# A shorter least time per unit in the clock that orders a four-layer kernel, and a bank kept for the front chain

## The chip, the cores and the metric

The kernel runs on one core of one Trainium2 chip. The metric is the device time of one execution in microseconds (us). A core has five engines that work side by side, each taking its instructions from a queue of its own: TensorE (PE in the profile; its weight loads are PEld), VectorE (DVE), ScalarE (ACT), GpSimd (POOL) and SyncE (SP, which here only issues DMAs).

## The reference

The input `x` is four images of 96 channels and 64 x 64 pixels. Four layers follow one another; each adds its result to what it got.

- Layer 0: group norm, layer norm, a projection to 2 x 192 channels, a 3 x 3 depthwise convolution, and then a selective scan over the 4096 pixels in four directions (rows, columns, and both backwards), with a state of 16 values per channel: `h = dA * h + d_t * u_t * b_t`, `y = sum(h * c_t)`. The four results are added, normed, multiplied by a gate and projected back to 96 channels.
- Layer 1: group norm and a deformable 3 x 3 convolution. A convolution gives for each pixel and tap an offset and a mask; the image is sampled there bilinearly (four corners), weighted, and multiplied by the 3 x 3 weights.
- Layer 2: over tokens, an FFT block (up to 192 channels, a transform over 4096 tokens, a product, ReLU, the inverse transform, and down to 96 channels), then a feed-forward block whose numbers are rounded to 8 bits.
- Layer 3: linear attention with six heads, and another such feed-forward block.

The recurrence is the heart of it: in `selective_scan` the state of each of 4 images x 4 directions x 192 channels x 16 values is carried through 4096 steps.

## The kernel before, in words

**The scan.** VectorE has an instruction that runs a recurrence along a row. The kernel cuts the work into 1536 *units*: for each image `b` and direction `k`, four pieces of 1024 pixels (`T`), and for each piece 24 units of eight channels x 16 state values on the 128 partitions. Images are taken one after the other; in images 1 to 3 the directions come in the order 1, 3, 0, 2, so that an image's last quarter is direction 2. A unit consists of: a load `da` of the step sizes (`fetch`, on ScalarE's DMA queue, five units ahead), their exponential (`decay`, L1014, ScalarE), two matmuls that spread the inflow into `db` in PSUM (`inflow`, L1020, TensorE), a product of `db` with `bc` (`enter`, L1034, VectorE), the scan into `hh` (`recur`, L1042, VectorE), a product of `hh` with the other half of `bc` (`weigh`, L1051, GpSimd), and matmuls that sum over the state into `py` (`total`, L1070, TensorE, for two units at a time). `py` is copied to `yb` and stored to DRAM as `y`.

**The side streams.** All else is written as Python generators that yield one *step* at a time, with its price for TensorE, VectorE, ScalarE and GpSimd. Two streams run beside the scan:

- `ends`: what comes before the scan and after sampling. It makes the scan's inputs for image 0 (`first`), then for images 1, 2 and 3 (`before`: convolution, projection, and `steps`, which makes step sizes and inflow), and then takes images 0 to 3 through layers 2 and 3 (`Layers23.image`; its store of `out` is L1833). An image enters layers 2 and 3 when `middle` has sampled it. `before(b)` has to be ready before the scan takes image `b`.
- `middle`: for each image `behind` (adds the directions of the scan, norm, gate, projection; it waits for the units of directions 3 and 2 that it reads, starts with L1134 on GpSimd and ends with L1180 and L1189), then `Layer1.image`: offsets and positions, and `sample`, which gathers 288 times from a table with GpSimd's indirect DMA (L1383), weighs the corners, transposes (L1416), multiplies by the weights and stores `x2` (L1439).

**Who sets the order.** The order is decided while the program is built, and each engine then runs its queue in that order. A `Clock` keeps for each engine a modelled time `ends[engine]`, and a scheduled time `due` of the scan. After each unit, `unit` adds `PACE` to `due`:

```python
    def now(self):
        return max(self.ends[DVE], self.due) if self.own is None else self.own

    def unit(self, scanned):
        self.due += PACE
        self.idle, self.beside = max(scanned, self.due), 0.0
```

Between two units the streams put in steps, `middle` before `ends` until the last image is sampled, for as long as `has_room` says that each engine of the step is at most `AHEAD` = (3, 3, 5, 7) us (PE, DVE, ACT, POOL) ahead of `now`, and while the VectorE work put beside a unit is under 6 us. When neither stream has a step that fits, the next unit is issued. A unit's own prices are 0.5 us for `inflow` and, for each two units, 1.5 us for `total` on TensorE (1.3 more for each eighth unit), 1.22 + 2.33 us on VectorE, 1.15 us on ScalarE for the exponential and 2.55 us on GpSimd; a gather is priced at 1.5 us of GpSimd. Where the inputs of the next image are not made yet, or when all units are over, a second mode (`alone`) takes steps without the scan.

Within a stream most stages are *pipelines*: `pipe` holds several chains (one for each chunk of pixels, say) in the order of their start and takes a step of the first chain that can go. The first of them is `active[0]`, the *front*. Three banks of PSUM are shared by the side streams while the scan runs (the scan has the other five); a step says with `holds` how many banks it keeps past its end, and with `new` that the next step will take a bank. `has_bank` asks whether one is free. After the scan its five banks become the own banks of `ends` (`own_banks`).

Of the kernel before, what the change touches and what calls it, by code (L numbers as in the profile page):

```python
# [186 lines left out]
def wait(us=0.0, **more):  # L187

    return Step((0.0,) * 4, us, **more)
# [10 lines left out]

MARGIN = 0.5

PACE = 4.5


class Clock:
# [19 lines left out]
# [4 lines that stand above are left out]
# [42 lines left out]
def pipe(net, chains, width, every=0, lane=None, **tiles):  # L272


    chains, active = iter(chains), []
    clock, known, more = net.clock, net.known, True
    end, free = clock.now(), tiles
    while True:
        if more and len(active) < width:
            steps = next(chains, None)  # L280
            if steps is None:
                more = False
            else:
                active.append(Chain(steps, clock.now()))
                continue
        if not active:
            break
        for n, chain in enumerate(active):
            if chain.new and not net.has_bank():
                continue  # L290
            if any(
                a.done <= chain.done + every
                for a in active[:n]
                if lane is None or (a.kind is lane) == (chain.kind is lane)
            ):
                continue
            if not all(free[tag] > 0 for tag in chain.takes):
                continue
            if clock.has_room(known.get((chain.kind, chain.done), (1.0,) * 4), chain.ready):
                break  # L300
        else:
            yield BLOCKED
            continue
        for tag in chain.takes:
            free[tag] -= 1
        clock.precede(known.get((chain.kind, chain.done), (0.0,) * 4))
        step = next(chain.steps, None)
        if step is None:
            net.hold(-chain.holds)
            active.remove(chain)  # L310
            end = max(end, chain.ready)
            continue
        for tag in step.frees:
            free[tag] += 1
        known[chain.kind, chain.done] = step.work
        chain.ready = clock.queue(step, chain.ready)
        chain.done += 1
        net.hold(step.holds - chain.holds)
        chain.holds, chain.new, chain.takes = step.holds, step.new, step.takes
        yield None  # L320
    yield wait(max(0.0, end - clock.now()))
# [38 lines left out]
class Net:  # L360
# [39 lines left out]
        own = self.own_banks and self.stream.own  # L400
        return (self.own_banks if own else self.psum).tile([128, CH], F32, name=name, tag="mm")[:p]

    def has_bank(self):
        if self.own_banks:
            return self.stream.held < (5 if self.stream.own else 3)
        return sum(stream.held for stream in self.streams) < 3

    def hold(self, n):
        self.stream.held += n
# [63 lines left out]
    def centred(self, x, cen, dst, key, pool, bias=None, groups=(0, 1)):  # L473
# [36 lines left out]
        def chains():  # L510
            for r in groups:
                for q in range(4):
                    yield chain(4 * r + q)
                yield sums(r)

        yield from pipe(self, chains(), 5, every=-99, sq=4, v0=-3, v1=-3)
        rstd = pool.tile([128, CH], F32, name=f"lns{key}", tag="lns", bufs=1)
        nw = pool.tile([128, CH], F32, name=f"lnw{key}", tag="lnw", bufs=1)
# [36 lines left out]
class Layer0:  # L555
# [54 lines left out]
    def first(self):  # L610
# [5 lines left out]
        with tc.tile_pool(name=f"l0u{b}", bufs=1) as up, tc.tile_pool(name=f"l0b{b}", bufs=1) as sm:  # L616
# [5 lines left out]
            with tc.tile_pool(name=f"l0a{b}", bufs=1) as big, tc.tile_pool(name=f"l0i{b}", bufs=1) as cp:  # L622
                pad = big.tile([C, PW, PW], F32, name=f"pad{b}", tag="pad")
                weights = self.conv_weights(b, cp)
                yield from self.normed_rows(b, x, pad)

                def rows_first():
                    yield self.conv(b, 0, pad, us, weights, cp)
                    for j in range(NCH):
                        if j + 1 < NCH:  # L630
                            yield self.conv(b, j + 1, pad, us, weights, cp)
                        yield self.projected(b, j, us, xp_a, xp_c, sm, xdbl, (0,), f"c{j}")
                        for ks in ((0,), (0, 2), (2,)):
                            yield self.steps(b, ks, j, us, dtw, sm, xdbl)

                tokens = {f"c{j}": 0 for j in range(NCH)}
                yield from pipe(
                    net, rows_first(), 6, every=2, lane=Layer0.conv.__code__,
                    ex=3, lw=2, rl=2, du=2, zt=1, **tokens,
                )  # L640

            def columns():
                for j in range(NCH):
                    yield self.projected(b, j, us, xp_a, xp_c, sm, xdbl, (1,))
                    for ks in ((1,), (1, 3), (3,)):
                        yield self.steps(b, ks, j, us, dtw, sm, xdbl)

            yield from pipe(net, columns(), 5, every=2, ex=3, lw=2, rl=2, du=2)

    def before(self, b):  # L650
# [1208 lines left out]
def layers23(net, x2, out):  # L1859
# [4 lines left out]
    with ExitStack() as ctx:  # L1864
# [37 lines left out]
        for goes in l0.scan():  # L1902
# [3 lines left out]
            if clock.own is not None:  # L1906
                clock.due = max(clock.due, clock.own + PACE)
                clock.idle = max(clock.idle, clock.due)
# [32 lines left out]
```

## Time and profile before

| what | value |
|---|---|
| time, median of three runs | 8518.56 us (8506.89 to 8540.53) |
| the profiled execution | 8585.65 us, of which its span is 8582.9 us |
| mean granted TensorE clock | 0.786 |
| busy: TensorE, VectorE, ScalarE, GpSimd | 76%, 79%, 57%, 65% of the span |
| first and last scan | 183 us and 7487 us |
| DMA: bytes, mean rate | 1608 MB, 187 GB/s |

The profiled execution is 0.8% above the median of the runs; its rows are used for durations and for the order of things. In a row of a group, the number after the bar is the busy time of all its instructions, then the mean duration of one in ns, then the idle time of the engine just before them and what ended most of that. In a row of waits, the numbers are the total in us, how often, and the longest. In a row of a timeline, the numbers are the start and the duration in us. In a row of a stretch, they are the ends of the stretch, its length, and the busy time of each engine with the number of instructions in brackets.

### The profile page before, as it was taken

The page shows a single profiled execution, that of the slowest core. Times are in us where ns is not written, and L with a number is a line of the kernel's source. Part 1 is how long each engine was busy: PE and PEld are TensorE (multiplying, and loading weights), DVE is VectorE, ACT ScalarE, POOL GpSimd, SP SyncE. Part 2 cuts the span into 40 slices and gives each one's busy share as a digit, 9 for nine tenths or more (in the row PEclk, how much of TensorE's full clock was granted, in tenths as well). Part 3 has the DMA queues.
Part 4 walks back from the last instruction along what each step waited for, and adds up shares of the span by engine and source line. Part 5 has one row for each costly group of instructions (what it writes and reads, how often), then busy time and mean ns, then how long its engine had stood idle before and what let it go on. Part 6 is the DMA issues. An engine that isn't in the chain of part 4 may idle for free.

```text
span 8582.9 us, 96776 instructions
## 1 busy us (share of the span) xinstructions
PE 6491.0 (76%) x31814; PEld 2822.5 (33%) x31848; DVE 6815.3 (79%) x5122; ACT 4923.9 (57%) x8979; POOL 5616.1 (65%) x4308
## 2 busy tenths in 40 slices
PE   6775877679767668777767889777788777887487
PEld 2211221122222223311223555214454332464274
DVE  2799889888799888688898888888888887727614
ACT  5664566546567767755566667554667774423124
POOL 1565567656579888666688887675788986517600
PEclk9766877679668779877777888778788877888698
DMA  3677678868789888876788989777898886734410
GB/s 97 168 198 193 167 196 221 212 159 204 189 215 249 224 228 222 202 190 187 205 229 225 235 227 228 172 174 188 223 243 219 210 212 168 176 103 131 131 56 20
DMA packets 773929, 1608.29 MB, mean 187 GB/s; under 512 B 264081, under 2 KB 355757, under 8 KB 771222
## 3 DMA queue, kind: packets, MB, share of 16 engines
q10 hardware_dynamic: 244224, 843.17, 38.4%
q1 hardware_dynamic: 455478, 532.37, 24.0%
q0 software_dynamic: 73728, 226.57, 9.9%
q8 instruction: 255, 4.18, 0.2%
q14 instruction: 244, 2.00, 0.1%
HBM read 1345.43 MB, written 256.29 MB: 187 GB/s over the span
## 4 chain that ended last, share of the span: by engine, by line
PE 35%; DVE 30%; DMA 9%; issue 9%; ACT 9%; POOL 4%; SPq 1%; ACTq 1%; another core or an unknown queue 1%; DVEq 0%; POOLq 0%
DVE hh L1042 15%; DVE db L1034 8%; PE pc L763 4%; PE py L1070 4%; PE ps L1416 3%; PE f L1510 3%; POOL hh L1051 3%; ACT g L1395 2%; PE pd L1432 2%; PE db L1020 2%; DMA da<-de 2%; ACT da L1014 2%; PE h L1551 1%; PE zp L1576 1%; DMA m<-in_dft 1%
## 5 line engine op out<-in xcount | busy, mean ns | idle before, releaser
L1051 POOL TENSOR_TENSOR hh<-hh,bc 128x1024 f32<-128x1024 f32 x1536 | 3670.2, 2391 | 348.3 <-DVE hh L1042 230.6
L1042 DVE TENSOR_TENSOR_SCAN hh<-da,st,db 128x1024 f32<-128x1024 f32 x1152 | 2701.3, 2345 | 205.3 <-PE py L1070 68.5
L1034 DVE TENSOR_TENSOR db<-db,bc 128x1024 f32<-128x1024 f32 x1536 | 1863.1, 1213 | 561.7 <-PE db L1020 542.2
L1014 ACT ACTIVATE da<-da,w_al 128x1024 f32<-128x1024 f32 x1536 | 1736.9, 1145 | 496.0 <-DMA da<-de 144.5
L1383 POOL DMA_INDIRECT g<-table,idx x1152 | 1190.6, 1034 | 410.9 <-issue 185.9
L1020 PE MATMUL db<-du,rep 24*128 24x512 bf16 x3072 | 697.7, 453 | 802.4 <-DVE hh L1042 752.2
L1070 PE MATMUL py<-hh,w_fold 128*32 128x512 f32 x6144 | 1115.9, 786 | 30.9 <-POOL hh L1051 18.0
L1395 ACT ACTIVATE g<-g,wt 128x96 f32<-128x96 f32 x3456 | 965.0, 364 | 133.5 <-PE py L1070 38.9
L1042 DVE TENSOR_TENSOR_SCAN hh<-da,db 128x1024 f32<-128x1024 f32 x384 | 877.1, 2284 | 73.9 <-PE py L1070 23.6
L1416 PE MATMUL ps<-w_ident,g 128*96 128x128 f32 x3744 | 690.5, 331 | 246.3 <-issue 122.2
L1020 PEld LDWEIGHTS <-rep 24*128 24x128 bf16 x3072 | 160.3, 93 | 1914.3 <-issue 1278.0
L851 POOL TENSOR_TENSOR lw<-lw,w 128x512 f32<-128x512 f32 x192 | 244.1, 1272 | 710.9 <-DVE w L849 668.5
L1416 PEld LDWEIGHTS ps<-w_ident,g 128*96 128x96 f32 x3744 | 501.6, 149 | 594.1 <-issue 211.2
L1049 POOL COPY st<-hh 128x1 f32<-128x1 f32 x1152 | 234.6, 204 | 648.4 <-DVE hh L1042 612.7
L763 PE MATMUL pc<-pad,wc 96*128 96x512 f32 x1152 | 570.8, 632 | 8.8 <-ACT st L1424 2.6
L1424 ACT COPY st<-ps 96x384 f32<-96x384 f32 x384 | 180.3, 472 | 578.9 <-PE ps L1416 421.5
L882 PE MATMUL pr<-ex,w_ident 128*128 128x512 f32 x384 | 299.7, 872 | 146.7 <-DVE ex L872 57.1
L840 PE MATMUL pd<-xd,w_dtw 103*64 103x512 f32 (+1 forms) x512 | 281.5, 818 | 71.2 <-DVE rl L853 26.9
L1432 PE MATMUL pd<-st,wdc 96*128 96x256 f32 x1152 | 323.0, 434 | 11.6 <-ACT st L1424 4.2
L763 PEld LDWEIGHTS pc<-pad,wc 96*128 96x128 f32 x1152 | 217.2, 199 | 311.8 <-issue 291.0
L1519 ACT COPY d<-f 128x512 f32<-128x512 f32 x192 | 111.3, 582 | 315.2 <-PE f L1510 282.3
L1070 PEld LDWEIGHTS py<-hh,w_fold 128*32 128x32 f32 x6144 | 160.9, 125 | 385.9 <-issue 293.3
(259 smaller groups left out, 8798.4 us busy)
## 6 DMA issues: line engine op xcount, KB each, us to landing
da<-de ACTq DMA_DIRECT2D x1536, 512.0 KB
du<-du SPq DMA_DIRECT2D x1536, 96.0 KB
bc<-bcd SPq DMA_DIRECT2D x128, 512.0 KB
y<-yb SPq DMA_DIRECT2D x384, 128.0 KB
de<-rl SPq DMA_DIRECT2D x128, 256.0 KB
m<-in_dft SPq DMA_DIRECT2D x128, 256.0 KB
ad<-y ACTq DMA_DIRECT2D x192, 128.0 KB
table<-pix SPq DMA_DIRECT2D x256, 96.0 KB
```

Of the source, the lines that this page charges most:

```text
L763: nc.tensor.matmul(pp, lhsT=wc[:, q, g * 128 : (g + 1) * 128], rhs=pad[:, r0 + dy : r0 + dy + NR, dx : dx + W], start=(q == 0), stop=(q == 8),
L882: nc.tensor.matmul(pr, lhsT=net.ident, rhs=ex, start=True, stop=False)
L1014: self.net.nc.scalar.activation(u.da, u.da, AF.Exp, scale=self.al[:, a : a + 1])
L1020: self.net.nc.tensor.matmul(db[:, h, :], lhsT=self.rep[64 * u.q + 32 * h : 64 * u.q + 32 * h + 24], rhs=u.du[64 * u.q + 32 * h : 64 * u.q ...
L1034: self.net.nc.vector.tensor_mul(u.db, u.db, u.bc[:, 0, :])
L1042: nc.vector.tensor_tensor_scan(u.along(u.hh), u.along(u.da), u.along(u.db), first, ALU.mult, ALU.add)
L1051: self.net.nc.gpsimd.tensor_mul(u.hh, u.hh, u.bc[:, 1, :])
L1070: nc.tensor.matmul(py[p0 : p0 + 32], lhsT=self.fold[:, u.i, :], rhs=hc[:, h * CH : (h + 1) * CH], start=u.sums["add"] is None and u.i == 0 ...
L1383: nc.gpsimd.indirect_dma_start(out=g[:, k, :], out_offset=None, in_=self.tables[b % 2], in_offset=bass.IndirectOffsetOnAxis(ap=idx[:, n : ...
L1395: nc.scalar.activation(pixel, pixel, AF.Identity, scale=wt[:, n, c : c + 1])
L1416: nc.tensor.matmul(pt[:, k, :], lhsT=g[:, k, c * C : (c + 1) * C], rhs=net.ident, is_transpose=True, start=(c == 0), stop=(c == corners - 1),)
L1432: nc.tensor.matmul(po, lhsT=wdc[:, k, :], rhs=st[:, k, :], start=(k == 0), stop=(k == 8))
```

## The change

`PACE` goes from 4.5 to 4.3 us. And `has_bank` takes a number: a chain that is about to take a new bank needs one free bank if it is the front of its pipeline or if the front holds a bank, and two free banks otherwise. Where a stream asks outside a pipeline, nothing changes.

```diff
-PACE = 4.5
+PACE = 4.3
...
         for n, chain in enumerate(active):
-            if chain.new and not net.has_bank():
+            if chain.new and not net.has_bank(1 + (n > 0 and not active[0].holds)):
                 continue
...
-    def has_bank(self):
+    def has_bank(self, n=1):
         if self.own_banks:
-            return self.stream.held < (5 if self.stream.own else 3)
-        return sum(stream.held for stream in self.streams) < 3
+            return self.stream.held + n <= (5 if self.stream.own else 3)
+        return sum(stream.held for stream in self.streams) + n <= 3
```

## The prediction

> **What bounds the kernel now.** I read the groups of instructions first, then the busy times of stretches, then the waits inside the scan, then the chain near the end. The groups give what one scan unit costs each engine:
>
> ```profile
> L1051 POOL TENSOR_TENSOR hh<-hh,bc 128x1024 f32<-128x1024 f32 x1536 | 3670.2, 2391 | 348.3 <-DVE hh L1042 230.6
> L1042 DVE TENSOR_TENSOR_SCAN hh<-da,st,db 128x1024 f32<-128x1024 f32 x1152 | 2701.3, 2345 | 205.3 <-PE py L1070 68.5
> L1034 DVE TENSOR_TENSOR db<-db,bc 128x1024 f32<-128x1024 f32 x1536 | 1863.1, 1213 | 561.7 <-PE db L1020 542.2
> ```
>
> VectorE carries 5441.5 us of these (1863.1 + 2701.3 + 877.1 of the other scan form): 3.54 us per unit that no order can remove. The stretches before and after the last unit, and the waits of VectorE in the first of them:
>
> ```profile
> 183.00:7490.00 7307.00, 5561.07 (x25901) 2230.07 (x25934) 6273.50 (x4298) 4523.06 (x8263) 5246.10 (x3981) 0.78 0.80 205
> 7490.00:8583.00 1093.00, 810.21 (x5653) 545.25 (x5651) 508.20 (x764) 306.85 (x594) 360.95 (x313) 0.80 0.31 89
> ```
> ```profile
> DVE db L1034 <- PE db L1020: 542.2, 234, 25.1
> DVE hh L1042 <- PE py L1070: 92.1, 89, 5.3
> ```
>
> The columns are PE, PEld, DVE, ACT, POOL, granted clock, DMA share. So a unit takes 7307 / 1536 = 4.76 us: 3.54 of its own VectorE work, 0.54 of the side streams' VectorE work ((6273.5 - 5441.5) / 1536), and 0.67 idle, most of it until TensorE, busy with side work queued in front, has made `db`. The scan is bounded by VectorE plus what the order puts in the way; 1093 us follow it. What they are:
>
> ```profile
> 7487.08 2.35 DVE L1042 TENSOR_TENSOR_SCAN hh<-da,st,db 128x1024 f32<-128x1024 f32 x1
> 7546.07 1.27 POOL L1180 TENSOR_TENSOR cc<-cc,zc 64x512 f32<-64x512 f32 x1
> 7667.07 1.02 POOL L1383 DMA_INDIRECT g<-table,idx  x1 [71.12 <-ACT d L1519]
> 8006.77 0.32 SPq L1833 DMA_DIRECT2D out<-t  x1
> 8165.38 0.30 SPq L1439 DMA_DIRECT2D x<-xo  x1
> ```
>
> Last scan, last product of `behind(3)`, first gather of image 3, image 2 finished by the stream `ends`, image 3 sampled by the stream `middle`; then 416 us of layers 2 and 3 on image 3. `middle` is the later by 159 us. The scan holds `middle` back at each image: sampling of image 0 ends at 3604, of image 1 at 5372, and `behind` then needs 41 and 38 us for its loads and four groups of 68 us (its first two groups of image 1 start at 3645 and 3713); that makes 3917 and 5682, yet it ends at 4023 and 5816, about 100 us after the last scan of its image (3920, 5725). For image 3 it is 7154 + 31 + 272 = 7457 against 7546. So `middle` has 106, 134 and 89 us of slack, and what shortens the scan shortens the whole until that is used up.
>
> [...]
>
> **The change, part by part.** No instruction, DMA or semaphore is added or removed; steps change places, with their DMAs on SP's, ACT's and POOL's queues.
>
> *PACE 4.5 to 4.3.* By the clock's prices a unit takes PE 0.5 + 1.5/2 + 1.3/8 = 1.41, DVE 3.55, POOL 2.55. What is left for side steps goes from 3.09 to 2.89 on PE (6.5% less), from 0.95 to 0.75 on DVE (21%), from 1.95 to 1.75 on POOL (10%). If side work per unit falls by some 10%, the 0.54 + 0.67 us per unit that it costs fall by **0.12 us**. Lower end: 6.5%, 0.08. Upper end: the full 0.20 of the clock. The scan shrinks by 1536 x 0.12 = 184 us (123 to 307), to end at 7303, and by 46 us per image.
>
> Sampling gets longer in units. The trace counts its units in the three windows of gathers:
>
> ```profile
> 2393.00:3551.00 1158.00, 594.78 (x256) 0.80 0.85 228
> 4236.00:5340.00 1104.00, 586.90 (x252) 0.81 0.90 230
> 6033.00:7133.00 1100.00, 600.95 (x258) 0.82 0.86 220
> ```
>
> On average 255 units of 4.39 us (the last columns: clock, DMA share, GB/s). If it is bound by latencies in the clock's time it needs 4.5/4.3 = 1.047 times as many, if by POOL's room 1.95/1.75 = 1.114; I take 1.08: 276 units of 4.27 us, 1178 against 1121, so **57 us more** per image.
>
> `middle` then: image 0 sampled at 3604 - 46 + 57 = 3615. `behind(1)` ends at the later of 3615 + 41 + 272 = 3928 and 4023 - 92 = 3931. Image 1 sampled at 5372 - 92 + 57 = 5337; `behind(2)` at the later of 5647 and 5816 - 138 = 5678. Image 2 sampled at 7154 - 138 + 57 = 7073; `behind(3)` at the later of 7376 and 7362. Image 3 is sampled at 8165 - 170 = **7995**.
>
> `ends` comes later. I take 5.5% less progress per unit (4.4% if bound by latency, 6.5% by PE). At the last unit it stands where it stood after 1536/1.055 = 1455 units, which was 7068; image 1 was stored at 7129, so 61 us are left. After the scan it is quicker: half of the Fourier stage took 193 us (7530 to 7723) against 303 and 325 within the scan, 1.6 times. So 61/1.6 = 38 for image 1, then image 2 whole: its norm 98/1.6 = 61, two halves 386, the rest as from 7723 to 8006, 283. That is 7303 + 38 + 730 = **8071**. Now `ends` is last, 76 us after `middle`; image 3 starts 94 us earlier than at 8165. I allow 4 for the fuller tail: **-90 us**. What is late next is thus image 2.
>
> *The last bank.* A chain behind the front may take a bank only if two are free or the front holds one; nothing costs time by itself. The bank that is kept too long now is that of `pd`: TensorE waited for `rl` (L853), which frees it, 26.9 + 22.5 + 19.0 + 9.7 + 9.1 + 5.2 = 92 us. That bounds a gain, of which perhaps half reaches VectorE's idle time: -40. A loss: gathers of a later chain start only with two banks free; sampling has 1152 gathers in all, and 3 us for one start in ten, on 384 chains, is 115 us over four images, some 40 of it past the slack. I take 0 and keep both ends.
>
> *DMA.* Its share in sampling is 0.90 at most; shorter units lift it to 0.90 x 4.39/4.27 = 0.925. The `da` loads are issued five units ahead (23.8 us, then 23.2). I cost this at nothing: that lead covers it. SP's queue carries the side streams' loads and stores between the scan's `du`, `bc` and `y`; with fewer side steps per unit, fewer stand before them. POOL has 1.04 gathers per unit of sampling (288/276) in place of 1.13 between its products: 2.39 + 0.15 + 1.04 x 1.03 = 3.6 of 4.27 us, so it doesn't become the bound of the units.
>
> Against the profiled execution: 8585.65 us (span 8582.9 and 2.75 around it) less 90 is 8495.7. The median of the runs is 0.9922 of it, so **8429**.
>
> **The rivals.** *Slower, because `ends` falls too far back.* Place: image 2 in layers 2 and 3. If `ends`, served after `middle`, loses POOL's 10% per unit, it stands at unit 1396, then about 6820; 309/1.6 = 193 us are left of image 1: 7303 + 193 + 730 = 8226, 61 later than now, 8580 by the median. It decides from 211 us left of image 1 at the scan's end (8165 - 7303 - 730 = 132, times 1.6), a loss of 8.2%. For it: `ends` gets what `middle` leaves, and had no pause to give away. Against it: PE's room shrinks by 6.5% only.
>
> *No change.* The units don't get shorter than 4.68, sampling takes 80 us more and the shift of `ends` eats the rest; within 43 us: 8519. For it: half of the idle time may be jitter that doesn't depend on the amount of side work.
>
> *Much faster.* The units fall by the whole 0.20: the scan ends at 7180, image 2 at 7948, 217 earlier: 8303. For it: where sampling is going on, a unit takes 4.39, close to the clock's 4.5. Against it: in the other stretches the measured unit is well above the clock's, so it isn't the clock that is felt there.
>
> *The change does nothing to the order*, because the clock is behind VectorE anyway: against it stands that side work and 3.55 us are 4.1 us of VectorE per unit, less than 4.5.
>
> **How the numbers follow.** About 0.5% (43 us) can be told from no change. Forecast, 45 to 160 us faster: 0.38. Much faster: 0.17. No change, with the order that does nothing: 0.20. Slower: 0.25. So faster 0.55, same 0.20, slower 0.25. The range reaches from the much faster case, 8315, to the slower one, 8575; the likeliest case alone spans 8360 to 8475.
>
> **What would show it.** Right: last scan near 7303 (unit 4.64 us), 265 to 285 units in each window of gathers, `behind(3)` ending later than 60 us after the last scan, and image 2's `out` store after image 3's last `x` store, with image 3's load right behind. Wrong: a last scan after 7400; windows of gathers under 260 units; image 2 stored before image 3 is sampled (the forecast's -90 then becomes -170); image 2 stored after 8165 (slower).

## The result, and the profile after

The changed kernel takes 8513.93 us (median of 20 runs) against 8542.0 us for the kernel before (20 runs beside it): a ratio of 0.9964, 95% interval 0.9951 to 0.9977. It is about 30 us faster, where 90 us had been forecast: the right side, a third of the size, and inside the range. One of the 20 runs of the changed kernel took 12083.6 us at a granted clock of 0.409 and is left out of the ratio. The profiled execution of the changed kernel took 8513.39 us (span 8511.6), so it is a usual one; the one of the kernel before, 8585.65 us, was 44 us above its median of 20 and above the slowest of them (8572.41).

The stretch up to the last scan and the one behind it, in the changed kernel (columns as before: PE, PEld, DVE, ACT, POOL, granted clock, DMA share, GB/s), and the longest wait of VectorE in the first:

```profile
188.00:7253.00 7065.00, 5315.88 (x24428) 2095.23 (x24429) 6179.49 (x4213) 4417.21 (x8054) 5178.15 (x3940) 0.78 0.82 209
7253.00:8512.00 1259.00, 1016.65 (x7141) 661.02 (x7135) 603.47 (x900) 392.06 (x755) 406.56 (x338) 0.84 0.34 92
```
```profile
DVE db L1034 <- PE db L1020: 489.0, 225, 25.0
```

The scan is 242 us shorter, the stretch behind it 166 us longer, and TensorE is now busy there for 1017 us instead of 810. A unit takes 4.60 us. The VectorE work of the units themselves is as it was, 5439 us in all; side work on VectorE fell from 0.54 to 0.48 us per unit ((6179.5 - 5439) / 1536), idle time from 0.67 to 0.58. The events at the end, from the timeline (start, duration):

```profile
7249.81 2.35 DVE L1042 TENSOR_TENSOR_SCAN hh<-da,st,db 128x1024 f32<-128x1024 f32 x1
7496.86 1.27 POOL L1180 TENSOR_TENSOR cc<-cc,zc 64x512 f32<-64x512 f32 x1
7610.96 1.02 POOL L1383 DMA_INDIRECT g<-table,idx  x1 [69.45 <-ACT d L1519]
8077.65 0.30 SPq L1439 DMA_DIRECT2D x<-xo  x1
8086.19 0.32 SPq L1833 DMA_DIRECT2D out<-t  x1
8093.46 0.30 SPq L1825 DMA_DIRECT2D t<-x  x1
```

Last scan, end of `behind(3)`, first gather of image 3, image 3 sampled, image 2 finished, image 3 loaded into layers 2 and 3. `behind(3)` now ends 247 us after the last scan (59 before), and `ends` is last by 9 us where `middle` had been by 159. The load comes 74 us earlier than in the profile of before (8093 against 8167), and the remaining 418 us are unchanged (416).

The units in the three windows of gathers (time, then VectorE's scans with their number); a unit takes 4.16 to 4.29 us there:

```profile
2390.00:3614.00 1224.00, 684.29 (x294) 0.78 0.91 238
4312.00:5488.00 1176.00, 638.35 (x274) 0.80 0.90 232
6089.00:7240.00 1151.00, 640.07 (x275) 0.83 0.90 225
```

### The profile page after: what moved, and what is told of

Read it like the earlier page. It is cut to its first block, busy times and chain, and to the rows that moved or that the text cites. A ratio compares the mean times of both kernels' runs of the same rounds, so it can differ in the third digit from the quotient of the medians.

```text
span 8511.6 us, 96951 instructions
## 1 busy us (share of the span) xinstructions
PE 6458.8 (76%) x31839; PEld 2805.7 (33%) x31839; DVE 6816.5 (80%) x5173; ACT 4906.0 (58%) x8935; POOL 5593.8 (66%) x4292
## 4 chain that ended last, share of the span: by engine, by line
PE 23%; DVE 15%; DMA 7%; ACT 5%; issue 5%; POOL 3%; SPq 1%; ACTq 1%; DVEq 0%; POOLq 0%
DVE hh L1042 7%; DVE db L1034 4%; PE f L1510 3%; PE ps L1416 3%; PE pd L1432 2%; PE py L1070 2%; DMA da<-de 2%; POOL hh L1051 2%; ACT g L1395 2%; PE h L1551 1%; PE db L1020 1%; ACT da L1014 1%; POOL g L1383 1%; DMA du<-du 1%; PE pc L763 1%
## 5 line engine op out<-in xcount | busy, mean ns | idle before, releaser
L1014 ACT ACTIVATE da<-da,w_al 128x1024 f32<-128x1024 f32 x1536 | 1736.3, 1145 | 488.6 <-DMA da<-de 197.0
L1070 PE MATMUL py<-hh,w_fold 128*32 128x512 f32 x6144 | 1090.8, 783 | 15.7 <-POOL hh L1051 7.7
L1395 ACT ACTIVATE g<-g,wt 128x96 f32<-128x96 f32 x3444 | 962.4, 363 | 171.4 <-PE py L1070 52.3
L1416 PE MATMUL ps<-w_ident,g 128*96 128x128 f32 x3735 | 679.9, 330 | 147.5 <-ACT g L1395 56.6
L1416 PEld LDWEIGHTS ps<-w_ident,g 128*96 128x96 f32 x3735 | 499.1, 148 | 478.7 <-ACT g L1395 166.4
L1432 PEld LDWEIGHTS pd<-st,wdc 96*128 96x128 f32 x1152 | 244.4, 220 | 110.4 <-issue 43.8
```

Of the source, the lines that this page charges most:

```text
L1014: self.net.nc.scalar.activation(u.da, u.da, AF.Exp, scale=self.al[:, a : a + 1])
L1070: nc.tensor.matmul(py[p0 : p0 + 32], lhsT=self.fold[:, u.i, :], rhs=hc[:, h * CH : (h + 1) * CH], start=u.sums["add"] is None and u.i == 0 ...
L1395: nc.scalar.activation(pixel, pixel, AF.Identity, scale=wt[:, n, c : c + 1])
L1416: nc.tensor.matmul(pt[:, k, :], lhsT=g[:, k, c * C : (c + 1) * C], rhs=net.ident, is_transpose=True, start=(c == 0), stop=(c == corners - 1),)
L1432: nc.tensor.matmul(po, lhsT=wdc[:, k, :], rhs=st[:, k, :], start=(k == 0), stop=(k == 8))
```

## The experiments

The experiments ran in five sets, each beside runs of the kernel before. Its median was 8591, 8556 and 8586 us in three sets on one chip, 8553 us in a fourth on another chip, and 8599 us in a fifth on a third chip. Ratios are to the kernel before of the same set. I call the second and the fourth set low (the result's own 8542 us is like them) and the other three high, and I compare within a set wherever I can.

**Both kernels once more, unchanged.** 

> The kernel before, profiled a second time, unchanged. Theory A (the execution first profiled was a slow one of its kind, 44 us above the median of twenty): span near 8540, image 3's load into layers 2 and 3 near 8130 rather than 8167. Theory B (its rows stand for the usual execution): load within 10 us of 8167, span within 15 us of 8583.

 

> The changed kernel, profiled a second time, unchanged. Theory A: last scan, image 2's store and image 3's last store within 20 us of 7250, 8086 and 8078, and the span near 8512. Theory B (which of the two streams is last is a matter of the execution): the order of image 2's store and image 3's last store turns round.

In this high set the kernel before took 8600.63 us and had image 3's load at 8183; the changed one took 8621.58 us, with the last scan at 7299, image 3 sampled at 8189, image 2 stored at 8198 and the load at 8205. `ends` was last by 9 us again, but neither theory's numbers came: the same program was 108 us longer than in its first profile. The stretch from image 3's first gather to its last store, in the changed kernel in a low set (`both43`, below), then in this execution:

```profile
7614.00:8080.00 466.00, 378.34 (x2515) 267.17 (x2513) 347.44 (x479) 140.86 (x283) 337.73 (x290) 0.84 0.50 148
```
```profile
7658.00:8189.00 531.00, 409.58 (x2492) 284.61 (x2490) 346.96 (x478) 140.69 (x283) 341.15 (x290) 0.77 0.44 130
```

The work on VectorE and GpSimd is the same, the time 65 us more, at a lower granted clock and a lower DMA rate. In the slower one the starts of the gathers have pauses of up to 25.8 us between them, 85 us in all of pauses over 4 us; in the quicker one, 21 us. The same stretch took 498 us in the first profile of the kernel before, 496 in the second. So the size of the change can't be read from one pair of profiles.

The traces show where the pauses come from. A gather needs one of six buffers `g`, which come free when TensorE has transposed what is in them (L1416), and the Fourier matmuls of `ends` (L1510) stand between the transposes in TensorE's queue. From the start of image 3's sampling on, and not only from its end, the builder serves `ends` before `middle`. The longest pause, from 7857 to 7883, ended only when the transposes behind 320 of these matmuls ran:

```profile
7861.90 19.90 PE L1510 MATMUL f<-w_idft,d 128*64 128x64 f32 x320
7881.74 2.44 PE L1416 MATMUL ps<-w_ident,g 128*96 128x128 f32 x18
```

Two rows of waits in this execution, then the same two in `both43`:

```profile
POOL g L1383 <- PE ps L1416: 74.5, 14, 24.9
PEld f L1510 <- issue: 30.7, 44, 2.1
```
```profile
POOL g L1383 <- PE ps L1416: 15.2, 5, 8.2
PEld f L1510 <- issue: 1.2, 4, 0.4
```

Here "issue" means that the engine waited for nothing that the profile shows. In this stretch the row of L1510 has at most 2.5 us in each of the nine profiles of kernels in low sets and in the result, and 16 to 34 us in each of the ten of high sets; the gathers' wait for L1416 is at most 18 us in the former and at least 27 us in the latter. The first profile of the kernel before, with 17.5 and 46.5 us, is like those of the high sets. What holds TensorE up there isn't shown.

**The two parts alone.** The pace alone is `PACE = 4.3` on the kernel before; the rule alone is the changed kernel with

```diff
-PACE = 4.3
+PACE = 4.5
```

> The shorter time per unit alone, with the old rule on banks. Theory A (the pace makes the gain): 25 to 35 us faster than before, last scan near 7250. Theory B (the bank rule makes it, and the pace alone costs what it brings): within 15 us of before or slower, though the last scan is near 7250 too. Theory C (any other order moves the time by some 20 us either way): anything between 30 us faster and 30 us slower.

 

> The bank rule alone, with 4.5 us per unit. Theory A: within 15 us of before, last scan near 7487. Theory B: 25 to 35 us faster than before. Theory C: anything between 30 us faster and 30 us slower, with the last scan within 20 us of 7487.

Pace alone: 1.0045 (1.0027 to 1.0062), slower, with the last scan at 7266. Rule alone: 0.9967 (0.9951 to 0.9983), with the last scan at 7478. Theory A was wrong and theory B came, so the forecast that the rule is worth nothing was wrong. This set was a high one, so both ran again in a low set, beside the whole change:

> The bank rule alone at 4.5 us, beside the other three on one chip. Theory H (the rule is worth 0.3% at 4.5): 0.995 to 0.9985 of before.

 

> The pace alone, beside the other three. Theory H (without the rule the shorter pace leaves ends too far back, and image 3 waits for it): 1.002 to 1.007 of before, image 2 stored after image 3 is sampled. Theory I (the pace is worth nothing either way, and the first set was unlucky): 0.998 to 1.002.

 

> The whole change, beside the other three. Theory H (with the rule, ends is 40 to 80 us less far back and the pace costs nothing): 0.994 to 0.9985 of before, within 0.002 of the rule alone.

| one set, before 8552.75 us | ratio | 95% interval | last scan | image 2 sampled | image 3 sampled | image 2 stored | image 3's load |
|---|---|---|---|---|---|---|---|
| rule alone, 4.5 | 0.9970 | 0.9959 to 0.9982 | 7492 | 7149 | 8122 | 7970 | 8123 |
| pace alone, 4.3 | 0.9997 | 0.9978 to 1.0017 | 7292 | 7219 | 8052 | 8111 | 8119 |
| both | 0.9956 | 0.9940 to 0.9972 | 7262 | 7276 | 8091 | 8100 | 8107 |

The rule gives 0.3% in both sets. The pace alone gives nothing in the low set, and costs 0.45% in the high one (theory I fits the first, theory H the second). On top of the rule the pace adds 0.14%, within the intervals. For that it ends the scan 230 us earlier. The table shows where that went. Pace alone: `middle` samples image 3 70 us earlier than with the rule alone, but `ends` stores image 2 142 us later, and image 3 waits for the later of the two:

```profile
8051.82 0.30 SPq L1439 DMA_DIRECT2D x<-xo  x1
8111.49 0.32 SPq L1833 DMA_DIRECT2D out<-t  x1
8118.76 0.30 SPq L1825 DMA_DIRECT2D t<-x  x1
```

(timeline of `pace_a`: image 3 sampled, image 2 stored 60 us later, load). Under the whole change `middle` is later than that at each image (by 72, 98, 57 and 40 us) and `ends` earlier (image 0 by 99, image 1 by 59, image 2 by 12): at 4.3 us the rule shifts progress from `middle` to `ends`.

Where does the rule act? In the scan alone. With the rule put only behind the scan, `net.has_bank(1 + (bool(net.own_banks) and n > 0 and not active[0].holds))`, the built program is that of the pace alone, row by row; with the rule only within the scan it is that of the whole change. These weren't run: they are the same programs.

**Other paces with the rule.** `PACE` is 4.3, 4.1 and 4.7:

> The changed kernel once more, on the chip that also runs other paces, so that they can be compared. Theory A (the bank rule makes the whole gain and the shorter time per unit adds nothing to it, since what the scan gives the stream ends takes): 20 to 40 us faster than before, as it was. Theory B (with the rule, the pace gives a gain of its own): over 40 us faster.

 

> The bank rule with 4.1 us per unit. Theory A (a shorter time per unit only moves side work behind the scan, where the stream ends is last): last scan 150 to 230 us earlier than at 4.3, images 0 and 1 stored later by 200 us or more, image 2 stored over 40 us after image 3 is sampled, and the whole 20 to 80 us slower than at 4.3. Theory B (the gain grows with the pace): 20 us or more faster than at 4.3.

 

> The bank rule with 4.7 us per unit. Theory A: the scan ends 150 us or more later than at 4.5, the stream middle waits for it at each image, image 2 is stored 200 us or more before image 3 is sampled, and the whole is 60 to 200 us slower than at 4.5. Theory B (at 4.5 the scan no longer follows the pace): within 40 us of 4.5.

At 4.3 the ratio is 0.9955 (0.9940 to 0.9970), at 4.1 0.9958 (0.9944 to 0.9972), at 4.7 1.0187 (1.0162 to 1.0211). Theory A came at 4.3 and at 4.7. Both theories on 4.1 were wrong, for a reason that neither had: its program is the same as that at 4.3. On every engine the two builds have the same instructions in the same order.

So with the rule, 4.3 is already below what the clock feels: `now` is the larger of VectorE's modelled end and `due`, and once `due` never leads, lowering `PACE` further changes nothing. At 4.7 the scan does bind: it ends at 7660, image 2 is stored by 7979, and `middle` is last alone:

```profile
7659.70 2.35 DVE L1042 TENSOR_TENSOR_SCAN hh<-da,st,db 128x1024 f32<-128x1024 f32 x1
8304.03 0.30 SPq L1439 DMA_DIRECT2D x<-xo  x1
8305.81 0.30 SPq L1825 DMA_DIRECT2D t<-x  x1
```

From 4.7 to 4.5 (7478 in `bank45`, of another set) the last scan comes 182 us earlier and the whole falls by 2.2 points of the ratio, some 185 us: about one for one. From 4.5 to 4.3 the last scan comes 230 us earlier and the whole falls by 0.14 points, 12 us. So the end waits for the scan at 4.7, and at 4.3 no longer.

In between, the rule with `PACE = 4.4`:

> The bank rule with 4.4 us per unit. At 4.5 with the rule middle was last by 151 us, at 4.3 ends by 9 us. Theory E: the scan ends between 7255 and 7478, the gap between the two streams lies between, and the whole is within 15 us of the changed kernel, since middle hardly gets earlier by giving room away. Theory G (the two are better balanced in between): 20 to 50 us faster than the changed kernel.

 

> The bank rule with 4.4 us per unit once more. Theory E (the gain is flat between 4.3 and 4.5, since what middle gains ends loses): 0.9945 to 0.998 of before. If 4.4 has a poor order of its own: 0.999 or more, as in the other set.

The ratios are 1.0014 (0.9996 to 1.0032) and 0.9999 (0.9980 to 1.0017), both in high sets, where the rule at 4.5 stood at 0.9967. So 4.4 is no better than before there and worse than 4.5, and theories E and G were both wrong. The gap between the streams doesn't lie between the two others either: `ends` is last by 20 us in both profiles (image 3 sampled at 8155 and 8128, image 2 stored at 8175 and 8148). 4.4 wasn't measured in a low set, and whether its order happens to be poor or the whole change does no better in a high set stays open: there the whole change has only the one execution, 8621.58 us against a median of 8591 (more on this below). The third profile of the kernel before fell in a high set too:

> The kernel before, profiled a third time, unchanged. Theory J (the pauses belong to the set of runs): where before takes under 8560 in this set, its gathers of image 3 have under 40 us of pauses over 4 us, and image 3's load comes 20 to 40 us earlier than 8167. Theory K (they are the kernel's own): 55 to 65 us of pauses and the load within 15 us of 8167 in any set.

Its gathers of image 3 had 46 us of pauses and the load came at 8182, but a low set was needed to tell theory J from K. For the kernel before that isn't settled.

**A stream helped.** In the changed kernel the clock's price of a gather was set to 1.2 us:

```diff
-                    yield cost(pool=1.5, wait=7.0 * (k == 2))
+                    yield cost(pool=1.2, wait=7.0 * (k == 2))
```

> The changed kernel with the clock's price of a gather at 1.2 us in place of 1.5; nothing else. Theory A (the streams middle and ends are within some 10 us of each other at the end, so that helping one alone brings little): 240 to 265 units per window of gathers in place of 275 to 294, image 2 sampled 40 to 100 us earlier, image 3's load into layers 2 and 3 set by image 2's store, the whole within 30 us of the changed kernel. Theory C (sampling's loss of room on GpSimd ate the gain): 40 to 90 us faster than the changed kernel.

The ratio is 0.9977 (0.9964 to 0.9990), slower than the whole change in the same set (0.9955), though the intervals overlap a little. The windows have 217 to 224 units, fewer than theory A said, and image 2 is sampled at 7038, 231 us earlier than in `both43` (7269); `ends` stores image 2 at 7964, 125 us earlier. And yet the load comes at 8110 instead of 8096, behind `middle` and not, as theory A had it, behind image 2's store. The scan gave back what the streams got:

```profile
7490.40 2.35 DVE L1042 TENSOR_TENSOR_SCAN hh<-da,st,db 128x1024 f32<-128x1024 f32 x1
8108.15 0.30 SPq L1439 DMA_DIRECT2D x<-xo  x1
8109.91 0.30 SPq L1825 DMA_DIRECT2D t<-x  x1
```

Its last scan is 235 us later than that of `both43` (7255). Here the scan's length and that of the stretch behind it trade against each other; their sum barely moves.

**Work left out of `ends`.** The layer 3 feed-forward block of image 2 was left out, in three kernels:

```diff
                 yield from self.attn.run(b, t)
-                yield from self.ffn3.run(b, t)
+                if b < 2:
+                    yield from self.ffn3.run(b, t)
```

> The kernel before, leaving out the last feed-forward block of image 2 (so that its output lacks that block); the order up to there is unchanged. The stream ends then finishes image 2 some 75 us earlier. Theory E (image 3 waits for the later of the two streams, and here that is middle by 159 us): 0 to 25 us faster than before, by contention alone. Theory F (the stretch behind the scan is bounded by the work of both streams together): 30 to 60 us faster.

 

> 4.3 us per unit with the old rule on banks, leaving out the same block of image 2. In the profile with the block, ends was later than middle by 60 us. Theory E: 60 to 90 us faster than with the block, so about 0.995 of the time before; image 3's load set by middle's last store. Theory F: 30 to 60 us faster than with the block, with or without a change of the stream that is last.

 

> The changed kernel, leaving out the same block of image 2. With the block, ends was later than middle by 9 us. Theory E: 10 to 35 us faster than the changed kernel, image 3's load set by middle's last store. Theory F: 30 to 60 us faster.

Without the block the kernel before stands at 0.9985 (0.9970 to 1.0001), 13 us. The pace alone stands at 0.9968 (0.9952 to 0.9983), against 1.0045 with the block in another high set: 0.77 points, 66 us. Its profile, the slowest of its 22 runs, doesn't show the load behind `middle` that theory E forecast: image 2 is stored at 8178, image 3 sampled at 8179, and the load follows at 8186. The whole change stands at 0.9971 (0.9957 to 0.9985), with no partner in a high set, so it ran again beside its partner in the low one:

> The whole change, leaving out the last feed-forward block of image 2, beside the other three. If image 3 still waits for ends in the usual execution: 0.0012 or more of before faster than the whole change. If ends and middle are level, so that helping one of them brings nothing: within 0.0012 of the whole change either way.

It stands at 0.9931 (0.9908 to 0.9953), against 0.9956 with the block: 0.25 points, 21 us (27 us by the medians, 8484.15 against 8511.16). The load now follows `middle`:

```profile
8064.58 0.30 SPq L1439 DMA_DIRECT2D x<-xo  x1
8066.36 0.30 SPq L1825 DMA_DIRECT2D t<-x  x1
```

That is theory E's order: 13, 66 and 21 us where `ends` had been 159 us early, 60 and 9 us late. Theory F fails at the kernel before, where its 30 us are outside the interval; at the other two the intervals would allow it. Nor need the later stream be all of it: in the last pair `middle` itself sampled image 3 at 8065 in place of 8091.

**High and low sets.** Three kernels ran in both kinds of set. The rule alone stands at 0.9967 in a high and at 0.9970 in a low one, the pace alone at 1.0045 and 0.9997, the whole change without the block at 0.9971 and 0.9931. So the gain of the rule at 4.5 held in both, while these two kernels at 4.3 lost 0.4 to 0.5 points in a high set; by an estimate from that loss and its 0.9956 in a low set, the whole change would gain next to nothing there. It fits the stretch of image 3's gathers: there the whole change has some 900 of the matmuls of L1510, the pace alone 1430, the rule at 4.5 only 130, and from a low set to a high one the stretch grew by 65, 81 and 22 us. No experiment took these matmuls out of the stretch.

No version with all the work beat the whole change by more than the intervals.

## Why the prediction was wrong, point by point

**The unit.** Forecast 4.64 us and the last scan at 7303; measured 4.60 and 7250. Side work and idle time did fall together (0.06 and 0.10 us per unit), by 13% where I took 10%. That the size came so near is in part luck: the sum takes the room that 4.3 us leaves beside a unit, and since 4.1 us gives the same program, it isn't the pace that sets this room.

**Sampling.** Forecast 276 units and 57 us more per image; measured 294, 274 and 275 units. From the first gather to the last store it took 1278, 1213 and 1175 us where it had been 1211, 1136 and 1121: 67, 77 and 54 more. That is near, but for image 0 outside the 265 to 285 units that were named as the sign.

**The progress of `middle`** is the first step that failed, in two terms: the 46 us that the scan was to give at image 0, and `behind`'s own speed. Measured less forecast, `middle` is late by 53 us at the end of image 0's sampling, 148 at the end of `behind(1)`, 187 when image 1 is sampled, 207 at the end of `behind(2)`, 191 when image 2 is sampled, 121 at the end of `behind(3)` and 83 when image 3 is sampled. The first 53 us arise because the gathers of image 0 began at 2390, 3 us earlier than before and not 46, and then took 10 us more than forecast. The next 95 are `behind(1)`. I took 68 us per group from its first two groups and so an own length of 313 us from the end of sampling. In the changed kernel sampling of image 0 ended at 3668, the four groups began at 3698, 3796, 3920 and 4005, and `behind(1)` ended at 4079, 411 us after sampling. The last group's inputs had been scanned by 3709, so it wasn't the scan. One short interval between two groups was no measure of the stage; what made the groups longer there, some 95 us each, wasn't tried. So of the 106 us of slack that I read at image 1 almost nothing was there: `behind(1)` took 411 us where it had taken 419. At the other two the slack was real, 361 us against 444 and 233 against 392. `middle` got 88 us earlier at the end where the sum said 170, and 32 of these are image 3's gathers, on which more below.

**The loss of `ends`** is the second. I took 5.5% less progress per unit. Image 0 was stored after 1161 units before (first row) and after 1256 in the changed kernel (second row), 8.2% more:

```profile
183.00:5763.00 5580.00, 2702.01 (x1161) 0.77 0.79 204
```
```profile
188.00:6068.00 5880.00, 2924.59 (x1256) 0.77 0.80 206
```

That is just the 8.2% from which the slower rival was to decide. It didn't, since the scan ended 53 us earlier than in that sum and image 2 took 686 us behind image 1 (7400 to 8086) instead of 730. At the scan's end 150 us of image 1 were left, not 38. The forecast of 8071 for image 2's store came near the 8086 of the profile by errors that cancel.

**The last bank at nothing** is the third, and most of what gain there is comes from it. Alone the rule is worth 0.3%, about 26 us. My bounds of 40 us either way held; the value was wrong, and so was the only mechanism I gave for a gain, shorter waits for `pd`'s bank. TensorE's waits for `rl` (L853) come in all to 102 to 105 us in the three profiles of the kernel before and to 122 and 124 us in the two with the rule alone: they grew. At 4.3 us the rule moves progress from `middle` to `ends`, which is last there. At 4.5 `middle` is last with and without it, and the gain shows at image 2: its gathers span 251 units with the rule and 258 without (images 0 and 1: 259 and 254 against 255 and 252), and from the first gather to the last store they take 1101 and 1093 us, against 1121 to 1142 in the three profiles of before. Which of the steps that changed places brings that wasn't shown.

**The base.** The sum was made against an execution 44 us above its median, and I scaled it by the ratio of the three runs then shown, whose median of 8518.56 us was 23 us under that of the 20. The two profiles differ by 74 us at image 3's load, near the forecast of 94; the medians differ by 28. A scale can't mend it, since the excess needn't be spread evenly: the gathers of image 3 took 32 us more in that profile than in the changed kernel's (498 against 466). By TensorE's waits there, the one profile is like those of the high sets and the other like those of the low ones, so the pair compares two conditions as well as two kernels.

**The DMA share and the `da` loads.** The share in sampling was forecast at 0.925; it is 0.90 to 0.91. The `da` loads were costed at nothing, as covered by their lead. Not all were: ScalarE waited 144.5 us for them in the kernel before (80 times) and 197.0 us in the changed one (112 times). VectorE's waits for the exponential that follows were 33.7 and 21.0 us, so they didn't grow.

**No instruction added or removed** was not quite so. Behind the scan the kernel does some steps in another form, on other engines (the corners of a tap weighted on VectorE in place of ScalarE, for one), so a step that moves there changes: L1395 on ScalarE has 3444 instructions instead of 3456, L1416 on TensorE 3735 instead of 3744. What that is worth wasn't measured.

**The rivals.** "No change" came nearest, and in part for its reason: `middle` and `ends` ate most of what the scan gave, but the units did get shorter than its 4.68 us. "The change does nothing to the order" was wrong as put, but its reason held from the other side: at 4.3 the clock follows VectorE and no longer the pace.

## What to carry to other kernels

Where a pacing parameter shares engines between a main loop and side streams, a shorter loop is a gain only while the loop is what the end waits for; move the parameter both ways, and look whether the built order still changes. Take the own speed of a stage from the place where it would have to run after the change, with its neighbours there, and not from its shortest interval. Before a forecast rests on a single profile, ask how far that execution lies from the median; for effects under 1%, compare kernels within one set of runs, and in more than one set.

## What the runs showed of the hardware

The engines ran their instructions in the order in which the program was built. In the profile of the changed kernel the source lines follow one another as in the program for 5173 instructions of VectorE, for the 8734 activations and copies of ScalarE, for the 4244 products, copies and gathers of GpSimd, and for all of TensorE's matmuls, 4931 stretches of one line each.

The kernel before had medians from 8542 to 8599 us in different sets of runs, 0.7% apart, and from 8556 to 8591 us in three sets on one chip, so the chip alone isn't the reason. The changed kernel's stretch with image 3's gathers took 466 us in one execution and 531 in another of the same program, at a DMA rate of 148 and 130 GB/s and a granted clock of 0.84 and 0.77. In the slower one the weight loads of L1510 waited 30.7 us there for nothing that the profile shows, in the quicker one 1.2 us, and the gathers waited 74.5 and 15.2 us for transposes in the same queue. Which of these is the cause and which the effect wasn't tried. The pace alone stood at 1.0045 in a high set and 0.9997 in a low one, further apart than their intervals: a ratio can depend on the set, too.
